# Order of the key chunks and reuse of two x tiles in an attention-plus-involution kernel on one core

## The chip, the cores and the metric

The kernel runs on one core of one Trainium2 chip. The metric is the device time in microseconds (us). Before the change three runs took 2714.2, 2718.0 and 2719.94 us, median 2718.0. The profile is of one further execution, whose own span is 2714.9 us.

## The reference, cut to what matters

Two layers work on an image batch x of shape (4, 512, 64, 64) in float32: four images, 512 channels, 4096 pixels each.

Layer 0 is attention over all pixels of an image, with 128 inner channels, and a residual:

```
q, k, v = wq·x + bq, wk·x + bk, wv·x + bv        # per image, 128 x 4096 each
attn    = softmax(q^T k)                          # 4096 x 4096
x       = wo·(v attn^T) + bo + x
```

Layer 1 is an involution (a convolution whose 7x7 weights are computed at each pixel), again with a residual:

```
o   = relu(s1·(W1·x) + b1)                        # 128 channels
w   = Ws·relu(sr·(Wr·o) + br) + bs                # 49 taps x 8 groups at each pixel
out = sum over the 49 taps of w * shifted o       # 16 channels share a group's weights
y   = s3·(W3·out) + b3 + x
```

The sum over keys inside the softmax, and the weighted sum of values, do not depend on the order in which the keys come.

## The kernel before

An image is cut into 8 chunks of 512 pixels (NCH = 8, CH = 512). A chunk of x is one tile of 128 partitions x 4 x 512 floats, 1,024 KB, from a pool of six buffers (L102). Everything lives in `fast_path`; a second path, `general_path`, is in the program for scores that overflow and is not run with these inputs.

For each of the four images two stages follow one another on TensorE (L600 to L609):

- `keys_values` (L392): for each chunk in the order 0 to 7, four matmuls `pk` give the keys and four matmuls `pv` the values; `turn` (L396) transposes the values of the chunk before (`pvt`, four small transposes). Each chunk of x is loaded into a tile called `xa`, dropped after the chunk, and each 128x512 matmul shows in the profile as two records of 0.43 us.
- `attention` (L541): for each chunk of queries, `queries` gives q (`pq`, four matmuls), then 32 steps of a score matmul `pss`, an exponential on ScalarE into `pt` (pool of five buffers, L104), a matmul `po` with the values, and an addition of `pt` into `pacc` on VectorE (the row sums, L588 to L594). This stage uses its own copy of the chunk of x, a tile called `xb`, which also takes the residuals and is what is stored at the end.

The rest of a chunk's life runs as generators whose steps are dealt out between these matmuls by `chores` (L239): `finish_block` (L445) divides by the row sums, multiplies by wo (`pwo`), adds the residual into `xb`, computes o (`p1`), and writes o transposed to DRAM (`pix`, L519); `pump` (L210) reads rows of it back as shifted windows (`ring`, L227); `involution` (L259) works through units of four image rows, two units to a chunk. For each unit TensorE makes the tap weights `pw` into a PSUM tile of which there is one (L247), VectorE multiplies (`prod`, L307, pool of four), GpSimd adds up (`acc`, L331 and L340). `turn_unit` (L346) transposes the sum (`pa`), and `close_chunk` (L376) multiplies by W3 (`py`), adds into `xb` (L383) and stores it (L389).

All loads of x, the ring, the writes of `pix` and the stores are issued from one queue, SyncE's, in order. The involution of an image lags its attention, so that the last units of one image (units 12 to 15, chunks 6 and 7) run during `keys_values` and the first chunk of `attention` of the next one.

What sets the order: the program gives the instructions in an order of its own, with a small running estimate of each engine's time (`until`, `pace`, `takes`) that decides where taps go. A scheduler then orders each engine's instructions once more when the program is built, by that order as a priority and by when it expects a buffer or an input to be there. [...]

Loads of x before: at the start of chunk c of `keys_values` that of chunk c + 1 is asked for (L405); at chunk 5 also `xb` of chunk 0 (L407); in `attention`, at step 14 of chunk c, `xb` of chunk c + 1 (L570); at step 8 of the last chunk, `xa` of chunks 0 and 1 of the next image (L572).

Of the kernel before, what the change touches and what calls it, by code (L numbers as in the profile page):

```python
# [8 lines left out]
F32 = mybir.dt.float32  # L9
# [6 lines left out]
P = 128  # L16
CT = C // P
CH = 512
NCH = N // CH
# [8 lines left out]
G = P // GC  # L28
CR = 32
NSLOT = (NTAP + 3) // 4  # L30


O_WK, O_WV, O_WQ, O_WO, O_W1, O_W3 = (i * 512 for i in range(6))
# [3 lines left out]
O_WS = O_WR + P  # L37
NWT = O_WS + NSLOT * P

# [35 lines left out]
def fast_path(  # L75
# [20 lines left out]
    nc = tc.nc  # L96

    def pool(name, bufs, **kw):
        return ctx.enter_context(tc.tile_pool(name=name, bufs=bufs, **kw))

    const = pool("const", 1)
    xpool = pool("x", 6)  # L102
# [4 lines left out]
    work2 = pool("work2", 2)  # L107
# [19 lines left out]
    x_r = x.rearrange("b (t p) n -> b p t n", p=P)  # L127
# [20 lines left out]
    def pe_us(us):  # L148
        nonlocal pe
        pe += us  # L150

    def takes(engine, us):
        free[engine] = max(free[engine], pe) + us
        return free[engine]

    def load_x(kind, b, c):
        xt = xpool.tile([P, CT, CH], F32, tag="x", name=f"{kind}_{b}_{c}")
        takes("dma", X_US)
        nc.sync.dma_start(xt, x_r[b, :, :, c * CH : (c + 1) * CH])
        return xt  # L160


    nc.scalar.dma_start(vec, vecs)
    nc.sync.dma_start(wt[:, :O_WV], wts[:, :O_WV])
    xa, xb = {(0, 0): xpool.tile([P, CT, CH], F32, tag="x", name="xa_0_0")}, {}
    for t in range(CT):
        nc.sync.dma_start(xa[0, 0][:, t, :], x_r[0, :, t, :CH])
    nc.sync.dma_start(wt[:, O_WV:O_WQ], wts[:, O_WV:O_WQ])
    xa[0, 1] = load_x("xa", 0, 1)
    nc.sync.dma_start(wt[:, O_WQ:], wts[:, O_WQ:O_WR])  # L170
    nc.gpsimd.memset(ones, 1.0)
    make_identity(nc, ident)
# [10 lines left out]
    def w_slice(off, t):  # L183
        return wt[:, off + t * P : off + (t + 1) * P]

    def v1(i):
        return vec[:, i : i + 1]

    def mm(o, lhsT, rhs, start=True, stop=True, shared=1):
        pe_us(rhs.free_size() * PE_COLUMN / shared)  # L190
        return nc.tensor.matmul(o, lhsT=lhsT, rhs=rhs, start=start, stop=stop)  # L191
# [47 lines left out]
    def chores():  # L239
        step(finishing, 1)  # L240
        step(closing, 1)
        pace()
# [131 lines left out]


    def close_chunk(b, c, off, n, acc):  # L376
        xt = xb[b, c][:, :, off : off + n]
        yield
        for t in range(CT):
            py = ps.tile([P, CH], F32, tag="mm", name=f"py_{b}_{c}_{off}_{t}")[:, :n]  # L380
            mm(py, w_slice(O_W3, t), acc[:, off : off + n])
            takes("dve", DVE_OP * n / CH)
            nc.vector.scalar_tensor_tensor(  # L383
                xt[:, t, :], py, v1(V_S3 + t), xt[:, t, :], ALU.mult, ALU.add
            )
            for _ in range(2):
                yield
        takes("dma", X_US)
        nc.sync.dma_start(out_r[b, :, :, c * CH + off : c * CH + off + n], xt)  # L389


    def keys_values(b):  # L392
        kt = kvpool.tile([P, N], F32, tag="k", name=f"k_{b}")
        vT = kvpool.tile([P, N // P, P], F32, tag="v", name=f"v_{b}")

        def turn(c, vs):  # L396
            pvt = ps1.tile([P, 4, P], F32, tag="acc", name=f"pvt_{b}_{c}")
            for j in range(4):
                nc.tensor.transpose(pvt[:, j, :], vs[:, j * P : (j + 1) * P], ident)
            pe_us(0.5)  # L400
            nc.scalar.copy(vT[:, 4 * c : 4 * c + 4, :], pvt)

        last = None
        for c in range(NCH):
            if c + 1 < NCH and (b, c + 1) not in xa:  # L405
                xa[b, c + 1] = load_x("xa", b, c + 1)
            if c == NCH - 3:  # L407
                xb[b, 0] = load_x("xb", b, 0)
            if b < 2 and c == 4:
                for rows in (slice(0, PAD), slice(PAD + H, None)):  # L410
                    nc.sync.dma_start(pix[b][rows].rearrange("r w c -> w r c"), zero)
                for cols in (slice(0, PAD), slice(PAD + W, None)):
                    nc.sync.dma_start(pix[b][PAD : PAD + H, cols, :], zero[:H])
            xt = xa.pop((b, c))
            pk = ps.tile([P, CH], F32, tag="s", name=f"pk_{b}_{c}")
            for t in range(CT):
                mm(pk, w_slice(O_WK, t), xt[:, t, :], t == 0, t == CT - 1)
                if t % 2:
                    chores()
            nc.scalar.activation(  # L420
                kt[:, c * CH : (c + 1) * CH], pk, AF.Identity, bias=v1(V_BK)
            )
            if last is not None:
                turn(c - 1, last)
            pv = ps1.tile([P, CH], F32, tag="po", name=f"pv_{b}_{c}")
            for t in range(CT):
                mm(pv, w_slice(O_WV, t), xt[:, t, :], t == 0, t == CT - 1)
                if t % 2:
                    chores()
            last = work2.tile([P, CH], F32, tag="q", name=f"vs_{b}_{c}")  # L430
            nc.scalar.copy(last, pv)
        turn(NCH - 1, last)
        return kt, vT

    def queries(b, c, off, n):
        xt = xb[b, c][:, :, off : off + n]
        pq = ps.tile([P, CH], F32, tag="mm", name=f"pq_{b}_{c}_{off}")[:, :n]
        for t in range(CT):
            mm(pq, w_slice(O_WQ, t), xt[:, t, :], t == 0, t == CT - 1)
        q = work2.tile([P, CH], F32, tag="q", name=f"q_{b}_{c}_{off}")[:, :n]  # L440
        nc.scalar.activation(q, pq, AF.Identity, bias=v1(V_BQ))
        return q


    def finish_block(b, c, off, n, po, sums):  # L445

        late = b == B - 1 and c >= NCH - 2
        name = f"{b}_{c}_{off}"
        xt = xb[b, c][:, :, off : off + n]

        def pause(us, steps):
            if late:
# [88 lines left out]
    def attention(b, kt, vT):  # L541
        blocks = [(c, 0, CH) for c in range(NCH)]
        if b == B - 1:

            blocks[-2:] = [(c, off, CH // 2) for c in (NCH - 2, NCH - 1) for off in (0, CH // 2)]

        steps = [(k, j) for k, (_, _, n) in enumerate(blocks) for j in range(N // P * n // CH)]
        qs, pts, pos, paccs = {}, {}, {}, {}
        qs[0] = queries(b, *blocks[0])

        def score(m):
            k, j = steps[m]
            n = blocks[k][2]
            pss = ps.tile([P, CH], F32, tag="s", name=f"pss_{b}_{k}_{j}")
            for i in range(CH // n):
                key = (j * (CH // n) + i) * P
                mm(pss[:, i * n : (i + 1) * n], kt[:, key : key + P], qs[k])
            pt = ptpool.tile([P, CH], F32, tag="pt", name=f"pt_{b}_{k}_{j}")
            nc.scalar.activation(pt, pss, AF.Exp)  # L559
            pts[m] = pt  # L560

        score(0)
        score(1)
        for m, (k, j) in enumerate(steps):
            c, off, n = blocks[k]
            nj = N // P * n // CH
            if j == 0:
                pos[k] = ps1.tile([P, CH], F32, tag="po", name=f"po_{b}_{k}")[:, :n]
                paccs[k] = ps1.tile([P, CH], F32, tag="acc", name=f"pacc_{b}_{k}")
            if j == 14 and (b, c + 1) not in xb and c + 1 < NCH:  # L570
                xb[b, c + 1] = load_x("xb", b, c + 1)
            if j == 8 and c == NCH - 1 and b + 1 < B:  # L572
                for i in range(2):
                    xa[b + 1, i] = load_x("xa", b + 1, i)
            if j == nj - 8 and k + 1 < len(blocks):
                qs[k + 1] = queries(b, *blocks[k + 1])
            if m + 2 < len(steps):
                score(m + 2)
            pt = pts.pop(m)
            for i in range(CH // n):  # L580
                key = j * (CH // n) + i
                mm(
                    pos[k], vT[:, key, :], pt[:, i * n : (i + 1) * n],
                    key == 0, key == N // P - 1,
                )
            takes("dve", DVE_OP)
            if j == 0:
                nc.vector.tensor_copy(paccs[k], pt)  # L588
            elif j < nj - 1:
                nc.vector.tensor_tensor(paccs[k], paccs[k], pt, ALU.add)  # L590
            else:
                sums = work1.tile([P, CH], F32, tag="sums", name=f"sums_{b}_{k}")
                nc.vector.tensor_tensor(sums, paccs.pop(k), pt, ALU.add)
                f = finish_block(b, c, off, n, pos.pop(k), sums)  # L594
                next(f)
                finishing.append(f)
            chores()
# [426 lines left out]
```

## Time and profile before

| | |
|---|---|
| three runs, median | 2718.0 us (2714.2 to 2719.94) |
| span of the profiled execution | 2714.9 us |
| TensorE busy | 2646.3 us, 97% |
| VectorE busy | 1871.6 us, 69% |
| GpSimd busy | 1821.3 us, 67% |
| ScalarE busy | 895.0 us, 33% |
| loads of x | 31 + 32 of 1,024 KB, and one in four pieces |
| DMA | 240.00 MB, 88 GB/s in the mean |

A busy time is the sum over a whole run whose stages have different limits. To see a stage, one reads the busy times in stretches of the span, and then the waits of one engine in a stretch. TensorE's share says only that it is nearly always at work; the few tens of microseconds in which it is not are what can be found in the stretches. The granted clock beside it is TensorE's, as a share of full speed.

### The profile page before, as it was taken

How to read it: one execution, taken by the hardware profiler on the slowest of the kernel's cores; microseconds unless marked ns; L12 is line 12 of the kernel's file. 1: busy time of each engine (PE TensorE's matmuls, PEld its weight loads, DVE VectorE, ACT ScalarE, POOL GpSimd, SP SyncE). 2: the span in 40 equal slices, each digit the busy share in tenths (PEclk: the TensorE clock that was granted, in tenths of full speed). 3: DMA queues.
4: the chain of work that ended last, by engine and by line, in shares of the span. 5: the costliest groups of instructions: out<-in, count | busy, mean ns of one | idle time of the engine just before them, and what ended most of it. 6: DMA issues, size and time to landing. Idle time of an engine off the chain costs nothing.

```text
span 2714.9 us, 22958 instructions
## 1 busy us (share of the span) xinstructions
PE 2646.3 (97%) x6932; PEld 1236.1 (46%) x6932; DVE 1871.6 (69%) x2609; ACT 895.0 (33%) x1495; POOL 1821.3 (67%) x1194
## 2 busy tenths in 40 slices
PE   9999999999899999999989999999979999999997
PEld 4444444444344444444434444444434444446863
DVE  0347777876565777777566678778746478787886
ACT  2333333332233333333223333333323333333320
POOL 0008788787841878878864488878876268787875
PEclk9999999999899999999989999999989999999999
DMA  7032333224504233333540433333461332322532
GB/s 244 14 72 59 89 90 77 73 72 126 154 32 103 58 89 89 89 89 90 142 123 20 85 72 74 90 89 89 119 181 54 77 78 68 80 56 61 113 90 67
DMA packets 108389, 240.00 MB, mean 88 GB/s; under 512 B 5272, under 2 KB 23904, under 8 KB 108128
## 3 DMA queue, kind: packets, MB, share of 16 engines
q1 hardware_dynamic: 108112, 238.35, 35.1%
q8 instruction: 56, 0.92, 0.1%
q14 instruction: 77, 0.63, 0.1%
q10 hardware_dynamic: 144, 0.10, 0.0%
HBM read 195.66 MB, written 42.77 MB: 88 GB/s over the span
## 4 chain that ended last, share of the span: by engine, by line
PE 89%; POOL 4%; DMA 3%; DVE 2%; issue 1%; SPq 0%; ACT 0%; POOLq 0%; DVEq 0%; ACTq 0%
PE pss L191 32%; PE po L191 32%; PE p L191 4%; PE py L191 4%; PE pwo L191 4%; PE pq L191 4%; POOL acc L331 3%; DMA ring<-pix 2%; PE pk L191 2%; PE pv L191 2%; PE pw L191 2%; DVE prod L307 1%; PE pr L191 1%; PE accp L191 1%; PE pa L357 1%
## 5 line engine op out<-in xcount | busy, mean ns | idle before, releaser
L331 POOL TENSOR_TENSOR acc<-acc,prod 128x768 f32<-128x768 f32 (+3 forms) x1059 | 1693.8, 1618 | 866.7 <-DVE prod L307 607.6
L191 PE MATMUL pss<-q,k 128*128 128x512 f32 (+1 forms) x2176 | 1052.4, 570 | 0.0
L191 PE MATMUL po<-pt,v 128*128 128x512 f32 (+1 forms) x2176 | 1047.5, 568 | 0.0
L559 ACT ACTIVATE pt<-pss 128x512 f32<-128x512 f32 x1024 | 611.4, 597 | 1198.4 <-PE pss L191 1169.9
L590 DVE TENSOR_TENSOR pacc<-pacc,pt 128x512 f32<-128x512 f32 x956 | 664.8, 695 | 482.5 <-ACT pt L559 473.8
L307 DVE TENSOR_TENSOR prod<-ring,pw 128x512 f32<-128x512 f32 (+3 forms) x1092 | 900.0, 850 | 125.2 <-POOL acc L331 80.6
L191 PEld LDWEIGHTS po<-pt,v 128*128 128x128 f32 x2176 | 410.9, 190 | 469.8 <-issue 446.1
L191 PEld LDWEIGHTS pss<-q,k 128*128 128x128 f32 x2176 | 403.9, 190 | 448.5 <-issue 434.7
L191 PE MATMUL py<-accT,wt 128*128 128x512 f32 (+1 forms) x264 | 135.9, 599 | 2.5 <-ACT accT L368 2.4
L383 DVE SCALAR_TENSOR_TENSOR xb<-py,vec,xb 128x512 f32<-128x512 f32 (+1 forms) x132 | 96.3, 731 | 59.6 <-PE py L191 57.2
L191 PE MATMUL pwo<-on,wt 128*128 128x512 f32 (+1 forms) x272 | 132.9, 576 | 3.8 <-DVE on L477 2.7
L340 POOL TENSOR_TENSOR acc<-acc 128x512 f32<-128x512 f32 x120 | 125.5, 1046 | 9.4
L191 PE MATMUL p<-xb,wt 128*128 128x512 f32 (+1 forms) x272 | 122.6, 576 | 7.3 <-DVE xb L484 7.3
L191 PE MATMUL pk<-xa,wt 128*128 128x512 f32 x256 | 123.7, 624 | 5.6 <-DMA xa<-x_dram 5.6
L500 ACT ACTIVATE xb<-xb,vec 128x512 f32<-128x512 f32 (+1 forms) x136 | 93.8, 694 | 95.9 <-PE p L191 92.1
L307 DVE TENSOR_TENSOR acc<-ring,pw 128x1024 f32<-128x1024 f32 (+1 forms) x84 | 78.9, 958 | 62.8 <-PE pw L191 62.2
L191 PE MATMUL pv<-xa,wt 128*128 128x512 f32 x256 | 116.8, 593 | 0.0
L191 PE MATMUL pq<-xb,wt 128*128 128x512 f32 (+1 forms) x272 | 116.0, 567 | 0.0
L484 DVE SCALAR_TENSOR_TENSOR xb<-pwo,bo,xb 128x512 f32<-128x512 f32 (+1 forms) x136 | 96.7, 715 | 18.2 <-PE pwo L191 17.0
L191 PE MATMUL pw<-wt,red 33*128 33x392 f32 x256 | 61.7, 560 | 21.8 <-DVE prod L307 21.7
L191 PEld LDWEIGHTS pk<-xa,wt 128*128 128x128 f32 x256 | 51.0, 202 | 69.9 <-issue 68.7
L191 PEld LDWEIGHTS p<-xb,wt 128*128 128x128 f32 x272 | 51.9, 192 | 66.9 <-issue 54.8
(58 smaller groups left out, 841.8 us busy)
## 6 DMA issues: line engine op xcount, KB each, us to landing
ring<-pix SPq DMA_DIRECT2D x30, 1344.0 KB, 15.2
ring<-pix SPq DMA_DIRECT2D x38, 896.0 KB, 12.0
xb<-x_dram SPq DMA_DIRECT2D x32, 1024.0 KB, 5.5
xa<-x_dram SPq DMA_DIRECT2D x31, 1024.0 KB, 5.4
out_dram<-xb SPq DMA_DIRECT2D x31, 1024.0 KB, 4.2
ring<-pix SPq DMA_DIRECT2D x66, 448.0 KB, 10.7
ring<-pix SPq DMA_DIRECT2D x8, 2240.0 KB, 24.2
pix<-o1t SPq DMA_DIRECT2D x60, 128.0 KB, 2.5
```

The source lines that it names most:

```text
L191: return nc.tensor.matmul(o, lhsT=lhsT, rhs=rhs, start=start, stop=stop)
L307: nc.vector.tensor_tensor(prod[:, :, p0 : p0 + n, :].rearrange("p t d (g c) -> p t d g c", g=G), image.rearrange("p t d (g c) -> p t d g c ...
L331: nc.gpsimd.tensor_tensor(acc[:, :, d0 : d0 + n, :], acc[:, :, d0 : d0 + n, :], prod[:, :, :n, :], ALU.add,)
L340: nc.gpsimd.tensor_tensor(acc[:, :, :n, :], acc[:, :, :n, :], acc[:, :, n : 2 * n, :], ALU.add)
L357: nc.tensor.transpose(pa[:, t, :], acc[:, t, 0, :], ident)
L383: nc.vector.scalar_tensor_tensor(xt[:, t, :], py, v1(V_S3 + t), xt[:, t, :], ALU.mult, ALU.add)
L484: nc.vector.scalar_tensor_tensor(xt[:, t, :], pw, bo[:, t : t + 1], xt[:, t, :], ALU.add, ALU.add)
L500: nc.scalar.activation(xt[:, t, :], xt[:, t, :], AF.Identity, bias=v1(V_B3 + t))
L559: nc.scalar.activation(pt, pss, AF.Exp)
L590: nc.vector.tensor_tensor(paccs[k], paccs[k], pt, ALU.add)
```

## The change

The order of the chunks in `keys_values` becomes 2, 3, 4, 5, 6, 7, 1, 0 (`KEYS`). There is one dictionary of x tiles, `xs`, in place of `xa` and `xb`. The tiles of chunks 1 and 0 are not dropped after their keys and values; `attention` takes them for its first two chunks of queries, so that these two are loaded once per image. The other six are loaded twice, as before. In `keys_values` the loads of the next two chunks are asked for at the start of a chunk, where it was one. The number of x loads falls from 64 to 56.

```
+KEYS = tuple(range(2, NCH)) + (1, 0)
+KEEP = 2
...
-    xa, xb = {(0, 0): xpool.tile([P, CT, CH], F32, tag="x", name="xa_0_0")}, {}
+    c0, c1 = KEYS[:2]
+    xs = {(0, c0): xpool.tile([P, CT, CH], F32, tag="x", name=f"x_0_{c0}")}
...
-        for c in range(NCH):
-            if c + 1 < NCH and (b, c + 1) not in xa:
-                xa[b, c + 1] = load_x("xa", b, c + 1)
-            if c == NCH - 3:
-                xb[b, 0] = load_x("xb", b, 0)
-            if b < 2 and c == 4:
+        for i, c in enumerate(KEYS):
+            for k in KEYS[i + 1 : i + 3]:
+                if (b, k) not in xs:
+                    load_x(b, k)
+            if b < 2 and i == 4:
...
-            xt = xa.pop((b, c))
+            xt = xs[b, c] if c < KEEP else xs.pop((b, c))
...
-                turn(c - 1, last)
+                turn(*last)
...
-            if j == 14 and (b, c + 1) not in xb and c + 1 < NCH:
-                xb[b, c + 1] = load_x("xb", b, c + 1)
+            if j == 14 and (b, c + 1) not in xs and c + 1 < NCH:
+                load_x(b, c + 1)
             if j == 8 and c == NCH - 1 and b + 1 < B:
                 for i in range(2):
-                    xa[b + 1, i] = load_x("xa", b + 1, i)
+                    load_x(b + 1, KEYS[i])
```

Lines that only rename (`xb[b, c]` to `xs[b, c]` in `close_chunk`, `queries` and `finish_block`) are left out.

## The prediction

> **What bounds the kernel now.** I read the table of engines first, then busy times in stretches of the span, then TensorE's waits in the stretches where it is not full, then the order of events there.
>
> ```profile
> PE 2646.3 (97%) x6932; PEld 1236.1 (46%) x6932; DVE 1871.6 (69%) x2609; ACT 895.0 (33%) x1495; POOL 1821.3 (67%) x1194
> ```
>
> TensorE (PE) is the bound; about 69 us of the span it stands still. The stretches (length, then busy time and count of PE, PEld, DVE, ACT, POOL; then the granted clock, DMA share, GB/s) say where:
>
> ```profile
> 0.00:70.00 70.00, 63.64 (x173) 30.06 (x174) 0.16 (x1) 15.39 (x25) 2.68 (x15) 1.00 0.71 247
> 70.00:600.00 530.00, 529.99 (x1295) 233.79 (x1294) 367.04 (x521) 190.65 (x315) 324.10 (x211) 1.00 0.27 64
> ...
> 660.00:730.00 70.00, 57.31 (x146) 25.43 (x147) 34.46 (x49) 16.76 (x28) 56.66 (x43) 0.85 0.66 181
> 730.00:1285.00 555.00, 554.99 (x1364) 245.12 (x1363) 404.38 (x570) 198.22 (x329) 380.80 (x246) 1.00 0.33 78
> ...
> 1285.00:1390.00 105.00, 91.11 (x241) 40.73 (x240) 62.09 (x78) 23.96 (x40) 90.40 (x60) 0.93 0.55 154
> ...
> 1940.00:2050.00 110.00, 95.94 (x247) 42.53 (x246) 62.56 (x79) 25.15 (x42) 89.56 (x60) 0.91 0.56 153
> ```
>
> Inside the attention TensorE never waits (529.99 of 530, 554.99 of 555). It loses time where one image gives way to the next, at about 660, 1320 and 1980 us, and there the clock also falls (0.85 to 0.93). The rest is the start (about 6 us) and the tail after 2600. TensorE's timeline at the first boundary (start, duration, what; in brackets the idle time and what ended it):
>
> ```profile
> 696.43 1.02 PE L191 MATMUL pq<-xb,wt 128*128 128x512 f32 x2
> 697.32 0.66 PE L399 MATMUL pvt<-ident,vs 128*128 128x128 f32 x4
> 697.81 2.74 PE L191 MATMUL pq<-xb,wt 128*128 128x512 f32 x6
> 707.83 1.68 PE L191 MATMUL pw<-wt,red 33*128 33x392 f32 x4 [7.27 <-DVE prod L307]
> 713.35 0.69 PE L357 MATMUL pa<-ident,acc 128*128 128x128 f32 x2 [3.84 <-POOL acc L340]
> 714.49 2.08 PE L191 MATMUL py<-accT,wt 128*128 128x512 f32 x2 [0.46 <-ACT accT L368]
> 716.36 5.37 PE L191 MATMUL pk<-xa,wt 128*128 128x512 f32 x8
> 721.57 3.60 PE L191 MATMUL pv<-xa,wt 128*128 128x512 f32 x8
> 725.00 1.02 PE L191 MATMUL py<-accT,wt 128*128 128x512 f32 x2
> ...
> 726.49 2.94 PE L191 MATMUL pss<-q,k 128*128 128x512 f32 x6
> ```
>
> The reader is to see that the keys and values of the last chunk (pk, pv) stand behind three waits of the involution: pw of unit 14 waits for VectorE's last product of unit 13, pa for GpSimd's sum, py for its copy. At 700.4 us TensorE had 7.3 us of work that needed none of this. VectorE had itself waited for the ring, which came late:
>
> ```profile
> 698.46 2.28 DVE L307 TENSOR_TENSOR prod<-ring,pw 128x256 f32<-128x256 f32 x5 [7.86 <-DMA ring<-pix]
> ...
> 706.66 1.11 DVE L307 TENSOR_TENSOR prod<-ring,pw 128x512 f32<-128x512 f32 x2 [0.80 <-POOL acc L331]
> ```
>
> Why is pk so late in the list? On SyncE's queue the load of xa 7 stands after xb 0 and after six ring loads:
>
> ```profile
> 679.42 0.37 SPq L159 DMA_DIRECT2D xb<-x_dram  x1
> 679.84 6.00 SPq L227 DMA_DIRECT2D ring<-pix  x6
> 685.88 0.60 SPq L159 DMA_DIRECT2D xa<-x_dram  x1
> 689.32 10.31 SPq L159 DMA_DIRECT2D xb<-x_dram  x2
> ```
>
> As I read it, the scheduler expected this load late and put the involution's matmuls first. The other two boundaries show the same list with waits of 7.15, 3.83, 0.46 and 7.32, 3.84, 0.46 us.
>
> [...] pk took 5.37 us after these waits against 3.60 elsewhere, and py 2.08 against 1.02 (both ends included). [...] the first wait is for data, not a buffer of x. [...] The loads of xb between 670 and 730 us took 6.4 to 22.9 us to land, against a median of 5.5 in the run. [...]
>
> **The change, part by part.** The built lists of both kernels differ only at the start, at the three boundaries and in the places of x loads; attention and tail have the same order.
>
> *Loads at a boundary.* Position by position on SyncE's queue, the new x tiles stand where the old ones stood: chunks 2 to 7 and 1 in the places of xa 0 to 6, and chunk 0 in the place of xb 0, before the ring loads and in the same kind of buffer (the one that the store of chunk 5 frees). xa 7 is gone. After the ring come chunks 2 and 3 for the attention where xa 7 and xb 1 stood; the xb 2 issued at about 699 us has no counterpart until a store has freed a buffer. So until then the DMA engines carry the same load, and I take the ring's landing at 698.4 us as unchanged. Asking two chunks ahead costs nothing: each load still waits for the buffer of three chunks before.
>
> *TensorE at a boundary.* Up to the second half of the fifth key chunk (677.7 us) both lists agree, with all their waits. Then the new one runs: values of the fifth, chunks 7, 1 and 0 complete, pq, and only then pw of unit 14, pss; pa of unit 13 comes after nine scores, two py after eleven and thirteen. Full-speed pieces, start to start in the timeline: pk or pv 3.43, pvt 0.44, so 7.30 per chunk. The old list reached pq at 696.43 after three chunks; the new one reaches chunk 0 then. Its x is needed at 696.4, where pq needed it; xb 0, issued at 679.42, landed after 6.4 us at the least, and pq did not wait for it. Chunk 0 ends at 703.7, pq and the last pvt at 707.7. pw becomes free when VectorE has finished unit 13, 707.8 us as before. New wait: 0.1 us.
>
> *After it.* pw takes 0.9 us, and q (0.69 us on ScalarE) is made beside it, so pss starts at about 708.8. At the start of the run, where nothing stood between pq and pss, the gap was about 0.9 us; I allow 0.3. GpSimd ends unit 13 at 713.25; the new pa stands after nine scores, at about 722, so the wait of 3.84 is gone.
>
> *The sum.* From pw to pss the old list takes 726.49 - 707.83 = 18.66 us. Its work at full speed: pw 0.86, pa 0.22, two py 1.72, pk and pv 6.86, pvt 0.44, together 10.1; the waits inside 4.3; so the lowered clock 4.26. Lost in all: 7.27 + 4.30 + 4.26 = 15.8. At the second boundary (1367.42 to 1385.67, 18.25) 7.15 + 4.29 + 3.86 = 15.3, at the third (2028.46 to 2047.28, 18.82) 7.32 + 4.30 + 4.42 = 16.0. Sum 47.1, less 0.4 per boundary of new waits: 46 us. The earlier wait of 2.45 us (p for VectorE at 661) stays.
>
> *Image 0.* Its first stage waits only 5.6 us for the first load and 0.7 for a copy; both remain. The 8 loads saved (1,024 KB at a median 5.4 us) lie beside full TensorE: nothing.
>
> *Does the involution keep up?* TensorE comes 15.6 us earlier into the attention while units 14 and 15 keep their clock time. GpSimd ends unit 14 at 743.4; the new list first needs it (pa of unit 14, after 26 scores) at 708.8 + 2.6 + 24 x 1.72 + 3.2 = 756. No wait. VectorE now has the products of unit 14 and 14 row-sum additions together: 1.3 + 12 x 0.62 + 7 x 0.88 + 14 x 0.72 + 2 x 0.67 = 26 us, which ends at about 735.5; TensorE reaches those steps at about 733. Five pt buffers allow a lag of about three steps, 5.2 us. So below nothing and above perhaps 3 us per boundary; I take nothing.
>
> Against the profiled span: 2714.9 - 46 = 2669. The runs' median lies 3 us higher: 2672.
>
> **The rivals.**
> (a) *The wait moves* (9 in 100). The ring lands later, or pw, now between queries and scores, waits for unit 13. Each microsecond then comes back[...]. With 5 us late: 5 + 4 lost of 15.6 at each boundary, 2718 - 3 x 6.6 = 2698. For it: pw and VectorE's end are only 0.1 us apart. Against: the same transfers run until 698 us.
> (b) *The attention's start is held by VectorE; slower* (3 in 100). A product waits for GpSimd, the additions behind it wait too, pt runs out. It decides only when VectorE lags by 15.6 + 5.2 = 21 us in the first chunk; at 25 us each boundary would lose 4, and the time would be 2730. Against: 26 us of work in 27 us.
> (c) *The involution is the true bound* (3 in 100): the time won comes back as waits at pa of unit 14 or in the tail, 2718. Against: GpSimd 381 of 555 us in an attention without one wait of TensorE.
> (d) *The change buys more* (4 in 100): without xb 2, and with fewer interleaved loads, units 14 and 15 also run earlier, and the 2.45 us wait goes as well: 2718 - 46 - 8 = 2664.
>
> **How the numbers follow.** Forecast 2672 us, 81 in 100, its own range 2666 to 2680 from the 6 us between the runs shown and 0 to 3 us of lag per boundary. The wide range takes in (d) at the low end and half of (a) at the high one: 2663 to 2692. Changes under 0.2% (5 us) can't be told from none. Slower by more: (b), 0.03, and 0.01 of unforeseen; same: (c), 0.03; faster: the rest, 0.93.
>
> **What would show it.** In the profile after: no wait of PE for prod, acc or accT at about 700 to 715 us over 1 us; granted clock in 660 to 730 near 1.00 apart from the wait at 661; pk and pv x8 at 3.60 throughout; TensorE busy less by about 13 us (only the lowered clock) and idle less by about 33. Wrong would be: a wait of pss or po for pt in the first chunk, pw waiting several microseconds, pk of chunk 0 waiting for its x, or waits in the attention where there were none.

## The result, and the profile after

The changed kernel took 2670.42 us (median of 4 runs, 2666.97 to 2671.78), the kernel before 2717.2 (4 runs, 2714.2 to 2719.94). The ratio is 0.9826 with a 95% interval of [0.9809, 0.9843]: 46.8 us less, where 46 were forecast. The engines of the changed kernel, as in the line shown of the kernel before:

```profile
PE 2635.7 (99%) x6932; PEld 1233.3 (46%) x6932; DVE 1865.3 (70%) x2609; ACT 894.5 (34%) x1495; POOL 1820.4 (68%) x1194
```

TensorE executes the same 6932 instructions. It stands still for 2669.5 - 2635.7 = 33.8 us, where it was 68.6, and is busy for 10.6 us less. The stretches around the three boundaries (length, busy time and count of PE, PEld, DVE, ACT, POOL, then granted clock, DMA share, GB/s):

```profile
660.00:730.00 70.00, 68.33 (x182) 31.07 (x183) 38.65 (x57) 22.17 (x37) 55.98 (x42) 0.98 0.59 151
...
1270.00:1375.00 105.00, 102.57 (x273) 46.11 (x272) 65.34 (x86) 29.30 (x49) 89.01 (x59) 0.98 0.49 134
...
1910.00:2020.00 110.00, 106.50 (x282) 48.06 (x281) 66.19 (x87) 30.52 (x52) 88.80 (x60) 0.98 0.52 138
```

Beside the old ones, 57.31 of 70, 91.11 of 105 and 95.94 of 110 us, TensorE is now busy for 11.0, 11.5 and 10.6 us more in stretches of the same length (the second and third begin 15 and 30 us sooner, as the image does), and the clock, which was between 0.85 and 0.93, is at 0.98. TensorE's timeline at the first boundary, in the changed kernel:

```profile
696.28 3.60 PE L194 MATMUL pk<-x,wt 128*128 128x512 f32 x8
...
700.15 3.60 PE L194 MATMUL pv<-x,wt 128*128 128x512 f32 x8
703.59 1.02 PE L194 MATMUL pq<-x,wt 128*128 128x512 f32 x2
...
708.42 0.93 PE L194 MATMUL pw<-wt,red 33*128 33x392 f32 x4 [0.71 <-DVE prod L310]
709.28 2.94 PE L194 MATMUL pss<-q,k 128*128 128x512 f32 x6
...
723.21 0.38 PE L360 MATMUL pa<-ident,acc 128*128 128x128 f32 x2
```

Keys and values of the last chunk (here chunk 0) fill the time in which the old list waited at pw. The scores start at 709.28 us instead of 726.49, and pa is reached at 723.21, when GpSimd, done at 713.88, has long finished. Of the wait at pw 0.71 us is left here; the two other boundaries have none and 1.0 us. Every other wait of TensorE was there before. The two profiled executions are 45.4 us apart.

### The profile page after: what moved, and what is told of

The parts are those of the page before. It is cut to its first block, busy times and chain, and to the rows that moved or that the text cites. A ratio compares the mean times of both kernels' runs of the same rounds, so it can differ in the third digit from the quotient of the medians.

```text
span 2669.5 us, 22935 instructions
## 1 busy us (share of the span) xinstructions
PE 2635.7 (99%) x6932; PEld 1233.3 (46%) x6932; DVE 1865.3 (70%) x2609; ACT 894.5 (34%) x1495; POOL 1820.4 (68%) x1194
## 2 busy tenths in 40 slices
DMA packets 104164, 231.60 MB, mean 87 GB/s; under 512 B 5144, under 2 KB 23776, under 8 KB 103904
## 3 DMA queue, kind: packets, MB, share of 16 engines
q1 hardware_dynamic: 103888, 229.96, 34.8%
## 4 chain that ended last, share of the span: by engine, by line
PE 92%; POOL 3%; DMA 2%; DVE 2%; issue 1%; SPq 0%; ACT 0%; POOLq 0%; DVEq 0%; ACTq 0%
PE pss L194 33%; PE po L194 33%; PE p L194 4%; PE pq L194 4%; PE py L194 4%; PE pwo L194 4%; POOL acc L334 3%; PE pk L194 2%; PE pv L194 2%; PE pw L194 2%; DMA ring<-pix 1%; PE pr L194 1%; DVE prod L310 1%; PE accp L194 1%; PE pp L515 1%
## 5 line engine op out<-in xcount | busy, mean ns | idle before, releaser
L386 DVE SCALAR_TENSOR_TENSOR x<-py,vec,x 128x512 f32<-128x512 f32 (+1 forms) x132 | 96.3, 731 | 60.7 <-PE py L194 58.6
L194 PE MATMUL p<-x,wt 128*128 128x512 f32 (+1 forms) x272 | 124.6, 584 | 7.3 <-DVE x L487 7.3
L503 ACT ACTIVATE x<-x,vec 128x512 f32<-128x512 f32 (+1 forms) x136 | 93.8, 694 | 97.9 <-PE p L194 94.2
L194 PE MATMUL pk<-x,wt 128*128 128x512 f32 x256 | 119.0, 605 | 5.1 <-DMA x<-x_dram 5.1
L194 PE MATMUL pv<-x,wt 128*128 128x512 f32 x256 | 116.8, 593 | 0.0
L194 PE MATMUL pq<-x,wt 128*128 128x512 f32 (+1 forms) x272 | 116.0, 567 | 0.0
L487 DVE SCALAR_TENSOR_TENSOR x<-pwo,bo,x 128x512 f32<-128x512 f32 (+1 forms) x136 | 96.8, 715 | 18.4 <-PE pwo L194 17.2
L194 PEld LDWEIGHTS p<-x,wt 128*128 128x128 f32 x272 | 52.6, 195 | 67.9 <-issue 55.5
L194 PEld LDWEIGHTS pwo<-on,wt 128*128 128x128 f32 x272 | 52.5, 194 | 61.9 <-issue 50.7
L194 PEld LDWEIGHTS pk<-x,wt 128*128 128x128 f32 x256 | 48.8, 194 | 64.8 <-issue 63.6
```

The lines of the kernel that those rows point to most:

```text
L386: nc.vector.scalar_tensor_tensor(xt[:, t, :], py, v1(V_S3 + t), xt[:, t, :], ALU.mult, ALU.add)
L487: nc.vector.scalar_tensor_tensor(xt[:, t, :], pw, bo[:, t : t + 1], xt[:, t, :], ALU.add, ALU.add)
L503: nc.scalar.activation(xt[:, t, :], xt[:, t, :], AF.Identity, bias=v1(V_B3 + t))
```

## The experiments

The theory is that time is won by what stands in front of the involution's waits in TensorE's list (the built list: the order in which the scheduler has put an engine's instructions). The trace of the kernel before shows that an instruction keeps its place behind such a wait: x of chunk 7, issued at 685.88 us, had landed after 23.6 us, at 709.5, and pk of that chunk started at 716.36, after TensorE had stood still for 3.84 us at pa and 0.46 at py. The rivals are that the reuse wins it, through 8 loads fewer (231.60 MB moved instead of 240.00), or that only one part of the change is needed.

**Two chunks ahead alone.** The kernel before, one edit:

```
-            if c + 1 < NCH and (b, c + 1) not in xa:
-                xa[b, c + 1] = load_x("xa", b, c + 1)
+            for k in range(c + 1, min(c + 3, NCH)):
+                if (b, k) not in xa:
+                    xa[b, k] = load_x("xa", b, k)
```

> The kernel before, with one edit: keys ask for x two chunks ahead. Order 0 to 7, no reuse, 64 loads. TensorE's built list at a boundary is then that of the changed kernel, chunk for chunk; the second copy of chunk 0 is loaded between the second and third pair of ring loads. Theory: pq needs that copy at about 703.7, issued at about 683 with some 18 us to land, so it just comes in time: 2672 us, 2666 to 2684. Rival (the gain comes from the reuse or the order of the chunks): 2717. Rival (the copy lands late behind the ring and pq waits): 2690 to 2705.

It took 2668.98 us (ratio 0.9827, [0.9810, 0.9843]), as fast as the whole change, with 240.00 MB moved. Its timeline of TensorE at the first boundary:

```profile
699.90 3.60 PE L191 MATMUL pv<-xa,wt 128*128 128x512 f32 x8
703.34 1.02 PE L191 MATMUL pq<-xb,wt 128*128 128x512 f32 x2
...
704.73 2.74 PE L191 MATMUL pq<-xb,wt 128*128 128x512 f32 x6
707.54 0.93 PE L191 MATMUL pw<-wt,red 33*128 33x392 f32 x4
```

This is the list of the changed kernel, with chunk 7 last instead of chunk 0: in the traces of the two kernels TensorE, VectorE, ScalarE and GpSimd each run the same sequence of instructions from start to end, but for the chunk that they work on. The second copy of chunk 0 for pq was in time; pw did not wait here. Neither the reuse nor the new order of the chunks is needed for the gain.

**Reuse and new order, one chunk ahead.** The changed kernel with `KEYS[i + 1 : i + 2]` in place of `KEYS[i + 1 : i + 3]`.

> The changed kernel with x asked for one chunk ahead instead of two; key order and reuse stay. The built lists of TensorE and SyncE are those of the changed kernel at the boundaries. Theory: the two-ahead part does nothing beside the reuse: 2670 us, 2666 to 2675. Rival (asking two ahead carries part of the gain in the changed kernel): 2685 or more.

It took 2668.27 us (ratio 0.9829, [0.9814, 0.9844]); the changed kernel, run again on the same chip, 2668.93 us (0.983, [0.9816, 0.9843]).

> The changed kernel once more, to compare the next one with on the same chip: 2670 us, 2666 to 2674.

The sequence on each of the four engines is again that of the changed kernel. So two parts of the change give the same thing, each by itself: x of the last key chunk takes the buffer that is freed first, and so is loaded ahead of the ring. With two chunks ahead it is asked for before the second copy of chunk 0, which took that buffer in the kernel before; with the reuse that copy is gone. Together they give it once. The reuse and the new order were not taken apart from each other.

**The last chunk ahead, without reuse.** The changed kernel with the two tiles dropped and loaded again, so that the first queries need a load after the keys:

```
-            xt = xs[b, c] if c < KEEP else xs.pop((b, c))
+            xt = xs.pop((b, c))
...
+        load_x(b, 0)
         turn(*last)
         return kt, vT
```

> The changed kernel without the reuse: key order 2 to 7, 1, 0 and two ahead, but chunks 1 and 0 are dropped after their keys and loaded again for their queries, chunk 0 asked for at the end of the keys; 64 loads. In the built list pw of unit 14 stands before pq and pa of unit 13 before the first score, since pq has to await its load. Theory: the last key chunk is still ahead of the waits, so most of the gain stays, but pw (to 707.8) and pa (to 713.3) hold TensorE: scores at about 714, 2688 us, 2682 to 2700. Rival (the reuse is nothing but fewer bytes, which are hidden): 2670. Rival (the reuse is the whole gain): 2717.

**The same place of the load in the kernel before**, by asking for the second copy of chunk 0 later:

```
-            if c == NCH - 3:
+            if c == NCH - 2:
                 xb[b, 0] = load_x("xb", b, 0)
```

> The kernel before, with one edit: the second copy of chunk 0 is asked for one chunk later, after chunk 7 of the keys. Nothing is reused, 64 loads. In the built list the load of chunk 7 then stands before the ring loads and pk, pv of chunk 7 before pw of unit 14; but pw and pa stand before the scores, with pq between. Theory (what counts is that the last key chunk comes ahead of the involution's waits): pw is reached at about 704 and waits to 707.8, pa to 713.3, scores start at about 714 instead of 726.5 (709.3 in the changed kernel), two py later: 2688 us, 2682 to 2698. Rival (the gain comes from the reuse, 8 loads fewer): 2717 as before. Rival (any gap filled brings the whole gain): 2670.

They took 2719.66 us (1.0011, [1.0002, 1.0019]) and 2719.73 us (1.0015, [1.0007, 1.0024]): nothing gained, where I had expected 2688 by the theory. The number is the one that the rival "the gain comes from the reuse" gave; but the kernel with two chunks ahead alone has no reuse either, and has the whole gain, so the cause has to be another. The two kernels here are one test rather than two: each of the four engines runs the same sequence of instructions in both. TensorE's timeline of the kernel without reuse:

```profile
708.25 1.68 PE L194 MATMUL pw<-wt,red 33*128 33x392 f32 x4 [3.10 <-DVE prod L310]
710.10 5.17 PE L194 MATMUL pq<-x,wt 128*128 128x512 f32 x8 [0.17 <-DMA x<-x_dram]
715.11 0.38 PE L360 MATMUL pa<-ident,acc 128*128 128x128 f32 x2
716.11 2.94 PE L194 MATMUL pss<-q,k 128*128 128x512 f32 x6 [0.62 <-ACT q L445]
...
734.53 2.07 PE L194 MATMUL pss<-q,k 128*128 128x512 f32 x2 [7.76 <-ACT pt L563]
```

and two lines of the other, where pq is held by the load as well:

```profile
707.50 0.93 PE L191 MATMUL pw<-wt,red 33*128 33x392 f32 x4 [3.04 <-DVE prod L307]
709.38 5.09 PE L191 MATMUL pq<-xb,wt 128*128 128x512 f32 x8 [0.95 <-DMA xb<-x_dram]
```

Up to the scores it went nearly as expected: they start at 716, 2 us later than forecast and some 7 us after those of the changed kernel. Then there is a new wait of 7.76 us, for an exponential. VectorE's timeline of the kernel without reuse tells why:

```profile
714.96 0.69 DVE L310 TENSOR_TENSOR prod<-ring,pw 128x512 f32<-128x512 f32 x1 [1.31 <-POOL acc L334]
...
732.23 0.95 DVE L310 TENSOR_TENSOR prod<-ring,pw 128x768 f32<-128x768 f32 x1 [0.93 <-POOL acc L334]
733.10 0.69 DVE L592 COPY pacc<-pt 128x512 f32<-128x512 f32 x1
734.11 0.95 DVE L310 TENSOR_TENSOR prod<-ring,pw 128x768 f32<-128x768 f32 x1 [0.33 <-POOL acc L334]
734.99 5.52 DVE L594 TENSOR_TENSOR pacc<-pacc,pt 128x512 f32<-128x512 f32 x7
```

All products of unit 14 but the last stand ahead of the first row-sum addition (pacc), most of them waiting for GpSimd; the five pt buffers stay occupied until 733 us. In the other kernel's trace, with the same sequence, the first exponential was done at 717.07 us (716.47 and 0.60), and VectorE came to its row-sum addition at 732.39, after standing still for 0.27 to 0.93 us at each product between. In the changed kernel the first pacc comes after the third product of the unit, and 13 more are spread between the others:

```profile
709.39 1.28 DVE L310 TENSOR_TENSOR acc<-ring,pw 128x512 f32<-128x512 f32 x2 [1.03 <-PE pw L194]
710.60 0.68 DVE L310 TENSOR_TENSOR prod<-ring,pw 128x512 f32<-128x512 f32 x1
711.20 0.69 DVE L591 COPY pacc<-pt 128x512 f32<-128x512 f32 x1
711.79 0.68 DVE L310 TENSOR_TENSOR prod<-ring,pw 128x512 f32<-128x512 f32 x1
...
734.48 0.94 DVE L310 TENSOR_TENSOR prod<-ring,pw 128x768 f32<-128x768 f32 x1
```

This is the mechanism of rival (b) of the prediction, in another kernel: as I read the lists, the scheduler took pq, and so the scores, to come late (in both kernels their load stands behind the ring), and dealt VectorE's work accordingly. The load really was late. It was issued at 685.74 us (685.05 in the other kernel) and landed 24.3 us later, at 710.0 (709.3), while the changed kernel starts pq at 703.59. That pq waited for it for only 0.17 us (0.95) is because TensorE had by then waited 3.10 us (3.04) at pw. So with this load pq could not have started before 710.0 in any order of TensorE's list, and that is nearly all of the 7 us by which the scores come later. The wait at pt comes on top.

To see whether this wait really ate the gain, the kernel without reuse was given more pt buffers (`pool("pt", 7)`), with no instruction moved:

> The kernel of e3_no_keep (2719.7 us) with seven pt buffers instead of five; the built lists of all engines are the same. There TensorE waited 7.8 us for pt at each boundary, because VectorE's list has nearly all products of unit 14 ahead of the first row-sum addition, and pt runs out. Theory (this is what ate the gain of moving the last key chunk): two more buffers let two more steps of 1.72 us run, the wait falls to about 4.4 us at each boundary, 10 us in all: 2709 us, 2704 to 2713. Rival (the 7.8 us are paid anyhow by GpSimd's sums, and only show up at pt): 2719.

It took 2708.13 us (0.9966, [0.9958, 0.9975]), 11.5 us less than with five (on another chip; with each compared with the kernel before on its own chip, 12.5). TensorE's wait for pt in it, and then in the kernel with five (us in all, how often, the longest):

```profile
PE pss L194 <- ACT pt L563: 12.0, 3, 4.2
```

```profile
PE pss L194 <- ACT pt L563: 22.8, 3, 7.8
```

Two buffers took 10.8 us off this wait, or 3.6 at a boundary, and the time fell with it. So this wait costs time. That the remaining 12 us would go the same way with more buffers was not tried.

**The reuse kept, the last chunk late.** The changed kernel, with one chunk ahead, and the attention's chunk 2 asked for before the last key chunk:

```
-            for k in KEYS[i + 1 : i + 3]:
+            for k in KEYS[i + 1 : i + 2]:
                 if (b, k) not in xs:
                     load_x(b, k)
+            if i == NCH - 3:
+                load_x(b, 2)
```

> The changed kernel with the reuse and the 56 loads kept, but x for the attention's chunk 2 is asked for before that of the last key chunk (chunk 0), which puts chunk 0 behind the ring loads. In the built list pw of unit 14 comes before pk of chunk 0, and the first half of pw of unit 15 before the first score; that one waits for the end of unit 14's products, at about 735 us. Theory (the place in TensorE's list decides): 11 us of wait at pw and a wait to about 735, scores 26 us later than in the changed kernel at each of three boundaries: 2745 us, 2720 to 2760, slower than before although two loads per image are saved. Rival (the reuse brings the gain): 2670.

It took 2755.44 us (1.0145, [1.0128, 1.0162]), 85 us more than the changed kernel, with the same 231.60 MB. Its timeline of TensorE:

```profile
706.24 1.68 PE L194 MATMUL pw<-wt,red 33*128 33x392 f32 x4 [9.57 <-DVE prod L310]
707.92 5.29 PE L194 MATMUL pk<-x,wt 128*128 128x512 f32 x8
...
733.20 1.64 PE L194 MATMUL pw<-wt,red 33*128 33x392 f32 x2 [12.38 <-DVE prod L310]
734.78 4.65 PE L194 MATMUL pss<-q,k 128*128 128x512 f32 x6
```

The last key chunk is again behind pw, and half of the pw of unit 15 has come before the first score as well, where it waits for all of unit 14. The scores start at 734.78 us, 25.5 us after those of the changed kernel; three boundaries make 77 of the 85 us.

**A version that beats both.** One wait that comes back at each boundary was left: that of p1 for VectorE's addition of the fourth quarter of x (2.43 us), because that addition stood behind five products in VectorE's list. In `finish_block` of the changed kernel one step is moved from before the fourth pwo to before p1:

```
-            for _ in range(t % 2 if late else 1 + (t != 1)):
+            for _ in range(t % 2 if late else (2, 1, 1, 3)[t]):
```

> The changed kernel, with finish_block giving up one step before its fourth pwo and taking one more before p1 (for all but the late chunks). VectorE's addition of the fourth quarter of x then stands two products earlier in its list, at about 656.5 instead of 660.2 us, and p1 no longer waits 2.43 us for it. Theory (this wait and the lowered clock after it are on the path, about 3.3 us at each boundary): 2660 us, 2656 to 2666. Rival (the ring or pw of unit 14 takes the wait over): 2670.

It took 2660.0 us (5 runs, 2659.41 to 2661.74), the changed kernel on the same chip 2668.93 (5 runs, 2667.64 to 2672.54). Against the kernel before, the ratio is 0.9797 [0.9783, 0.9810]. VectorE's addition in it, and then p1 on TensorE with the wait behind it:

```profile
655.86 0.74 DVE L487 SCALAR_TENSOR_TENSOR x<-pwo,bo,x 128x512 f32<-128x512 f32 x1
```

```profile
657.83 1.88 PE L194 MATMUL p<-x,wt 128*128 128x512 f32 x4
660.43 1.12 PE L194 MATMUL py<-accT,wt 128*128 128x512 f32 x2 [0.72 <-DVE x L386]
```

p1 waits no longer and runs at full clock (1.88 us, 2.57 in the changed kernel). A wait of 0.72 us at py takes a part of it over. Of the 10 us forecast, 8.9 came.

## Why the prediction was right

VectorE in the changed kernel, from the end of its wait for the ring to its last products of unit 13:

```profile
699.02 2.28 DVE L310 TENSOR_TENSOR prod<-ring,pw 128x256 f32<-128x256 f32 x5 [7.97 <-DMA ring<-pix]
...
707.26 1.10 DVE L310 TENSOR_TENSOR prod<-ring,pw 128x512 f32<-128x512 f32 x2 [0.81 <-POOL acc L334]
```

- *The waits.* The three waits of the involution (7.27, 3.84 and 0.46 us at the first boundary) shrank to 0.71, none and none. At the other two boundaries pw waits for nothing and for 1.05 us, which is as much as came of rival (a). The 4 us that it adds to a lateness of 5 were the author's estimate; the prediction's sum has 3.86 to 4.42 us of lowered clock at a boundary. The step "pw becomes free when VectorE has finished unit 13, as before" held: that end came at 708.36 us in place of 707.77 (second line above).
- *TensorE's arrival.* Forecast for pq and the last pvt: done at 707.7; pw started at 708.42 after 0.71 us of wait, so 707.7.
- *The sum.* 46 us forecast, 46.8 measured. The mechanism can be held against it boundary by boundary: from a matmul ahead of the boundary to one behind it, the changed kernel needs 15.1, 15.3 and 15.0 us less. The losses worked out in the prediction, 15.8, 15.3 and 16.0, less the waits at pw that are left, 0.71, none and 1.05, come to 15.1, 15.3 and 15.0. The split is less exact: 34.8 us of idle time (forecast about 33) and 10.6 of busy time (about 13). The idle time has 0.6 us from the first load and 1.4 from after TensorE's last matmul, which the change does not touch. The busy time is the lowered clock, seen in pk (mean 605 ns, 624 before) and py (584, 599 before), whose instructions are the same; it falls short because p and the py behind it at the second boundary ran at lowered clock in the changed kernel and not before (1.7 us: four records of p took 3.68 us in place of 1.98). That the total comes within 1 us is in part luck: these pieces cancel, and single runs of one kernel lie 5 us apart.
- *The first chunk of the attention.* VectorE's products and additions were forecast to end at about 735.5. The last product ended at 735.42 (734.48 and 0.94, the last of the lines of the changed kernel's VectorE under the experiments), and TensorE never waited for pt.
- *The ring.* Forecast unchanged; VectorE's product that waited for it started at 699.02 us (first line above), 698.46 before.
- *Loads saved.* Forecast at nothing, and shown to be: with the same lists 240.00 MB moved took 2668.98 us and 231.60 MB 2670.42, and with another list 231.60 MB took 2755.44.
- *What the prediction did not say* is that asking two ahead would be enough alone. It called this part free beside the reuse, which held (2668.27 without it), but did not see that it is a second way to the same list.
- *Its rival (b)* was given 3 in 100, by the length of VectorE's work. The experiments show that this rests on how VectorE's list is interleaved, not on the sum of its work: with nearly the same work the wait is 0 or 7.8 us. For the changed kernel the list was known, and the estimate stood.
- *Its reading of the first wait* needs a correction. The prediction says that this wait is "for data, not a buffer of x". It is for a buffer, though not of x: pw of unit 14 waits for the one PSUM tile of pw, which VectorE's last product of unit 13 sets free, as it says itself further down. A second pw tile, the direct answer to that wait, was not tried.

## What to carry to other kernels

When a scheduler orders the engines, read a change of loads in the built lists: what mattered here is which independent work stands in front of a wait, on every engine that works through a list in order, and not how many bytes are saved. The smallest edit with the whole gain is the one that asks two chunks ahead. Work out when each engine arrives at a wait and when that wait ends. Here the work moved ahead of it (7.3 us) is as long as the wait (7.27), and nearly the whole wait was won, along with the two behind it and the time at lowered clock. Then look for what else the same load has moved: two kernels had the last key chunk ahead of the waits on TensorE and their scores 10 us sooner than before, and lost all of that again, mostly to a wait for VectorE (7.76 and 7.85 us at the first boundary) and the lowered clock after it (the next two records of pss took 2.07 us, against 1.02 before the wait).

## What the runs showed of the hardware that I had not expected

*Short waits and the clock.* TensorE's clock fell after one wait of 2.4 us and not after another. The wait for VectorE's addition in the kernel before, at the first and at the second boundary:

```profile
661.11 3.04 PE L191 MATMUL p<-xb,wt 128*128 128x512 f32 x4 [2.45 <-DVE xb L484]
...
1322.52 1.98 PE L191 MATMUL p<-xb,wt 128*128 128x512 f32 x4 [2.44 <-DVE xb L484]
```

The same four records took 3.04 us after the one and 1.98 after the other. The records of the granted clock in the traces of the kernel before and of the changed kernel show a pattern. In each of the two, all stretches at half clock (0.50 granted; seven and five of them, 3.41 to 17.07 us long) begin a whole number of steps of 3.41 us apart, and last a whole number of such steps, but for the stretch that the program's end cuts. So each of the two traces can be divided into cells of 3.41 us. Of the cells at full clock ahead of TensorE's last matmul, all 8 in which it stood still for 2.12 us or more in sum were followed by a cell at half clock, and none with 1.18 us or less; of the four in between, those with 1.32 and 1.35 us were, those with 1.36 and 1.85 us were not. The first wait above lies in one cell whole (658.48 to 661.90 us, 2.45 us still; the next cell has 0.50 granted); the second is divided over two, with 0.59 and 1.85 us, and the clock stayed at 1.00. In these traces what such a wait cost thus went with where it fell as well as with how long it was. In the kernel before with its load moved the clock also fell late: pw took 0.93 us right after a wait of 3.04 us, as long as in the changed kernel after 0.71 us, and it was the pq behind it that ran slowly (5.09 us for eight records, three of them at 1.06 to 1.22 us against 0.59 at full speed).

*Loads behind the ring.* In that kernel the three loads of x issued behind six ring loads took 20.0 to 24.3 us to land, against a median of 5.6 us for this copy of x over the whole run.
